# First layer of a graph network: edge attributes in 512-byte parts, products in two row tiles of 64, PSUM in units of four tiles

## The chip, the cores and the metric

The kernel runs on one core of one Trainium2 chip. The metric is device time in microseconds (us) of one execution. The engines are named as in the profile: PE is TensorE's matrix multiplication and PEld its loading of weights, DVE is VectorE, ACT is ScalarE, POOL is GpSimd, SP is SyncE. Each of them works through its own queue in order, and SP, ACT and POOL also issue DMA transfers from their queues.

## The reference

Four layers follow one another on 6250 nodes of 256 features, with 106250 edges that are sorted by their destination (dst):

```
edge_index = stack([src, dst])
x = x + L0_gnn(layernorm(x), edge_index, edge_attr_256)
x = x + L0_ffn(layernorm(x))      # attention over a fixed graph picks 2 of 4 experts
x = x + L1_gnn(layernorm(x), edge_weight, src, dst)
x = x + L1_ffn(layernorm(x))

def L0_gnn(x, (row, col), edge_attr):
    h = relu(concat([x[row], edge_attr], axis=1) @ W1 + b1)      # 106250 x 512 by 512 x 256
    agg = segment_sum(h, col) / max(count(col), 1)
    return relu(concat([x, agg], axis=1) @ W2 + b2)
```

All of it is float32. The change concerns nearly nothing but L0_gnn, which the text calls the first layer.

## The kernel before

The first layer splits W1. The node half of the product, y = layernorm(x) @ W1a + b1, is computed once for each node and stored in DRAM (y_dram), between the start and about 110 us. The edge half runs in a loop over edges: h = relu(y[src] + edge_attr @ W1b), and the sums per destination come from products with matrices of ones and zeros (equals) that compare the edge's destination with the node's number.

**Tiling.** There are T = 49 windows of P = 128 nodes. As the edges are sorted, a window's edges lie together: from a start found at run time (`start_of`, L1087) the kernel takes CW x P = 18 x 128 = 2304 edge rows, in 18 tiles of 128. They are worked through in NG = 3 groups (TURNS, L949) of G1 = 6 tiles, in two runs of NT = 3 tiles (k = g and k = g + 3). So there are 147 groups, and the loop over them (L1738 to L1771) is the first layer's loop.

**The steps of a group.** `load_attr` (L1494) loads the attributes of the 6 tiles into `ea` with 8 DMAs of 96 KB, 4 from SP's queue and 4 from ACT's. Each fills 32 partitions with pieces of 64 features, 256 bytes. Three `ea` buffers exist (L1455). `load_sources` (L1603) issues six indirect gathers from POOL, one for each tile, of y rows by source index into `h`, a ring of four groups. `turn` (L1611) transposes `ea` on DVE in blocks of 32 x 32 into `et`, so that features lie on partitions. `hidden(q, j)` (L1619) multiplies two tiles of `et` with W1b (`w1b`) over 128 rows in two steps of accumulation, into `ph`, a PSUM tile of 6 x 256 floats a partition (three banks, two such buffers). A float32 matmul shows as two in the trace, so a group has 24 ph matmuls. `join` (L1629) adds PSUM and `h` on DVE (L1632) and takes the relu on ACT (L1633), once a group. `add_up` (L1636) forms the sums per node with matmuls of 32 columns each (L1652, tile `pe`), four of which lie side by side in the array; a window's three turns show 12, 16 and 24 of them.

**The end of a window.** `end_of` (L1658 to L1710) is a generator whose stages are spread over the iterations that follow the window: division by the count (`rc` on DVE, ACT L1665), two transposes on PE (`pt<-ident,o`, L1158) that ACT empties (L1159), four products with W2, the residual and the layer norm on DVE and ACT, two transposes of the result into `b_all` (again L1158 and L1159), and products with `wgx` for the next layer's attention, which ACT copies into `gtab` and `a_dst` (L1704 to L1706). All of these use one PSUM buffer, `pt`.

**The order.** `Ordered.pin` (L28) ties every instruction of the loop to the one before it on the same engine, so that each engine keeps the program's order. One iteration q issues, in this order: join(q-1), hidden(q, 0), side work (sorting of edges for the middle layers), add_up(q-2) and a stage of end_of, gathers (LATE1 tiles of q+1, EARLY1 tiles of q+2), turn(q+1), hidden(q, 2), side work, the equality matrices, hidden(q, 4), the index work of later windows (`load_windows`, L1182), and at the end load_attr of up to q+4. The first groups' load_attr is issued in the stage before (L1557).

**Indices.** `load_windows` writes the gathers' indices. For windows from the third on, rows outside the window get an index of 8192 or more (FAR), and every gather is issued with a test (`bounds_check`) that skips such rows.

**Later stages.** Attention and experts run from about 1625 to 3080 us, the last layer's loop of gathers (`hg`, 831 of them) to the end. The last layer's pool opens at L2455 with 17 loads of weights on SP's queue (L2466 to L2489), ahead of the last stores and loads of the layer before it that use that queue.

Of the kernel before, what the change touches and what calls it, by code (L numbers as in the profile page):

```python
# [9 lines left out]
F32 = mybir.dt.float32  # L10
# [18 lines left out]
class Ordered:  # L29

    def __init__(self, tc):
        self.tc, self.last = tc, {}
        self.traced = tc.nc.cur_bb.bb.instructions
        self.at = self.traced[-1]

    def pin(self):
# [6 lines left out]
        for i in reversed(new):  # L43
            if i.engine in self.last:
# [867 lines left out]
def kernel(ctx: ExitStack, tc: tile.TileContext, a: dict, out: bass.AP):  # L912
# [25 lines left out]
    FAR = 8192.0  # L938
# [56 lines left out]
    with ExitStack() as fast:  # L995
# [180 lines left out]
        def gather(dst, table, idx, **more):  # L1176
# [5 lines left out]
        def load_windows(b, pool):  # L1182
# [47 lines left out]
            if first:  # L1230
                V.tensor_copy(flat3(src1[:, 0:first, :, :]), g[:, 0:first, :])
            far = g[:, first:, :]
            V.scalar_tensor_tensor(
                far, flat3(inside[:, first:, :, :]), -FAR, far, op0=OP.mult, op1=OP.add
            )
            V.tensor_scalar(
                flat3(src1[:, b * TB + first : (b + 1) * TB, :, :]), far, FAR, None, op0=OP.add
            )
# [92 lines left out]
        def make_keys(ix):  # L1331

            n = C2 // KS
            for k in range(KS):
                src, dst = (v.bitcast(I32)[:, k * n : (k + 1) * n] for v in (key, order))
                d, ok, last = (
                    ix.tile([P, n], t, name=f"key{i}", bufs=1) for i, t in enumerate((F32, F32, BF16))
# [110 lines left out]
        with ExitStack() as layer:  # L1448
# [8 lines left out]
            def load_weights(pool):  # L1457

                w1b = wp.tile([P, 2, D], F32, name="w1b")
                for k in range(4):  # L1460
                    rows = a["L0_gnn_W1"][D + 2 * k * Q : D + 2 * (k + 1) * Q, :]
# [32 lines left out]
            def load_attr(q):  # L1494

                w, g = groups1[q]
                ea = wea.tile([P, 2, NT * 4, 2 * Q], F32, name="ea")
                r = start_of(w, mybir.EngineType.Activation)
                rows = a["edge_attr_256"][bass.ds(r, WE), :]
                for i, k in enumerate((g, g + NG)):  # L1500
                    part = rows[k * NT * P : (k + 1) * NT * P, :]
                    for c in (0, 2, 1, 3):
                        (SY if c < 2 else SC).dma_start(
                            ea[c * Q : (c + 1) * Q, i, :, :],
                            part[:, 2 * c * Q : 2 * (c + 1) * Q].rearrange(
                                "(m p) d -> p m d", p=Q
                            ),
                        )
                return ea


            with (
# [11 lines left out]
                for t0, t1 in parts0:  # L1524
# [32 lines left out]
                    if b >= 4:  # L1557
                        ahead[b - 4] = load_attr(b - 4)
# [3 lines left out]
            with (  # L1562
                tc.tile_pool(name="e1", bufs=2) as wk,
                tc.tile_pool(name="y0", bufs=1) as wy,
                tc.tile_pool(name="ph1", bufs=2, space=PSUM) as psh,
# [4 lines left out]
                ring = [wy.tile([P, G1, HS], F32, name=f"h{i}") for i in range(4)]  # L1570
                for h in ring:
                    V.memset(h[:, :, D:WS], 1.0)
# [27 lines left out]
                def rows_of(q):  # L1600
# [1249 lines left out]
```

## Time and profile before

| what | value |
|---|---|
| runs | 4302.15, 4324.18, 4345.13 us; median 4324.18 |
| profiled execution | 4332.62 us, its span 4330.8 us, granted PE clock 0.824 |
| first layer's loop | about 110 to 1600 us |
| attention and experts | about 1625 to 3080 us |
| last layer's loop | 3080 to 4331 us |
| busy over the span | PE 3249.3, PEld 2483.7, DVE 2191.0, ACT 1189.9, POOL 2298.0 us |
| DMA packets | 698661, 423.05 MB, 532488 of them under 512 bytes |
| attribute loads | 588 on SP and 588 on ACT, 96 KB each |

Times in the views are microseconds from the span's start unless marked ns. A line of groups gives the source line, the engine and operation, the tile that is written and those that are read, the shapes and the count; then busy time and mean duration; then the idle time of the engine just before these instructions, and what ended it. "remote" and "another core or an unknown queue" mark a releaser that the profile can't name; "issue" is time in which an engine waited for nothing that the profile shows. In a timeline, the bracket is the idle time before a piece and its releaser. ACTq and SPq are the queues of ACT and SP issuing DMAs. PEclk is the clock granted to PE as a share of full speed.

### The profile page before, as it was taken

Reading aid. Unit: us, or ns where it says so; the run is one execution under the profiler, and the core shown is the slowest. Engines: PE = TensorE matmul, PEld = TensorE weight load, DVE = VectorE, ACT = ScalarE, POOL = GpSimd, SP = SyncE. Lnnn points to the kernel's source line nnn. Section 1 sums busy time; section 2 is a strip of 40 time slices with the busy share of each in tenths; the row PEclk is TensorE's granted clock in tenths of the full one; section 3 lists DMA queues with packets and bytes.
Section 4 is the critical chain, followed back from the end, with each engine's and each line's share of the span. In section 5 each row is a group of like instructions: output and inputs, shape, how many; then the busy total and the mean of one; then the engine's idle time right before and its main releaser. Section 6 shows DMA issues by size and latency. Waiting matters only on the chain.

```text
span 4330.8 us, 59911 instructions
## 1 busy us (share of the span) xinstructions
PE 3249.3 (75%) x18517; PEld 2483.7 (57%) x18517; DVE 2191.0 (51%) x6402; ACT 1189.9 (27%) x2200; POOL 2298.0 (53%) x2720
## 2 busy tenths in 40 slices
PE   7778788878888885777887878685356776777787
PEld 5556566656666664556666656564244454555566
DVE  6566566666565543555555454575123333333344
ACT  3122222222222231334544444464001111111133
POOL 2655555655666544345454444432666666665551
PEclk9889898989999897888898988896566777667687
DMA  6666667766776642222323232333111111111110
GB/s 187 156 145 148 144 151 155 159 140 152 160 168 152 149 119 61 63 63 81 97 77 104 68 101 70 87 103 93 46 46 51 47 50 50 51 50 47 49 49 20
DMA packets 698661, 423.05 MB, mean 98 GB/s; under 512 B 532488, under 2 KB 641092, under 8 KB 698332
## 3 DMA queue, kind: packets, MB, share of 16 engines
q1 hardware_dynamic: 366524, 188.25, 16.1%
q0 software_dynamic: 88512, 171.34, 16.1%
q10 hardware_dynamic: 243296, 59.53, 7.0%
q8 instruction: 150, 2.46, 0.2%
q14 instruction: 179, 1.47, 0.1%
HBM read 382.75 MB, written 42.50 MB: 98 GB/s over the span
## 4 chain that ended last, share of the span: by engine, by line
PE 49%; another core or an unknown queue 17%; issue 14%; DVE 9%; ACT 4%; POOL 3%; DMA 2%; ACTq 1%; SPq 1%; DVEq 0%; POOLq 0%
PE ph L1164 22%; PE py L1164 10%; PE pe L2710 5%; PE pe L1652 3%; PE pt L1164 3%; PE po L2031 2%; POOL hg L1177 1%; DVE et L1614 1%; POOL h L1177 1%; PE pt L1158 1%; DVE h L1632 1%; PE pa L1954 1%; DMA h<-y_dram,src 1%; DVE eq L2687 1%
## 5 line engine op out<-in xcount | busy, mean ns | idle before, releaser
L1177 POOL DMA_INDIRECT h<-y_dram,src x882 | 896.8, 1017 | 672.7 <-issue 318.4
L1177 POOL DMA_INDIRECT hg<-hp_dram,src x831 | 785.8, 946 | 489.4 <-issue 217.9
L1177 POOL DMA_INDIRECT sg<-gat_dram,src x612 | 595.3, 973 | 729.1 <-DVE pay L1991 308.5
L1164 PE MATMUL ph<-w1b,et 128*128 128x256 f32 x3528 | 885.2, 403 | 44.0 <-issue 29.6
L1164 PEld LDWEIGHTS ph<-w1b,et 128*128 128x128 f32 x3528 | 690.9, 201 | 224.7 <-issue 131.0
L1164 PE MATMUL py<-w,hh 128*128 128x256 f32 x1568 | 452.3, 427 | 96.6 <-issue 43.7
L2710 PEld LDWEIGHTS pe<-eq,hg 128*128 128x128 f32 x2036 | 380.5, 258 | 250.7 <-issue 157.2
L2710 PE MATMUL pe<-eq,hg 128*128 128x96 f32 (+15 forms) x2036 | 391.7, 338 | 147.2 <-issue 83.5
L1164 PE MATMUL ph<-b_all,w 128*128 128x256 f32 (+1 forms) x1600 | 470.4, 434 | 12.1 <-issue 11.0
L1632 DVE TENSOR_TENSOR h<-ph,h 128x1536 f32<-128x1536 f32 x147 | 258.3, 1757 | 421.2 <-remote 184.3
L2687 DVE TENSOR_SCALAR eq<-px,dst,ew 128x96 f32<-128x96 f32 x831 | 261.9, 368 | 311.0 <-remote 137.0
L1164 PEld LDWEIGHTS py<-w,hh 128*128 128x128 f32 x1568 | 305.6, 209 | 159.3 <-issue 58.5
L1633 ACT ACTIVATE h<-h 128x1536 f32<-128x1536 f32 x147 | 218.4, 1486 | 623.0 <-DMA ea<-in_edge_attr_dram 273.7
L1164 PEld LDWEIGHTS ph<-b_all,w 128*128 128x128 f32 x1600 | 324.1, 219 | 63.1 <-issue 21.0
L2009 DVE TENSOR_SCALAR E<-nodes,bits 128x256 bf16<-128x256 bf16 (+5 forms) x612 | 187.2, 338 | 181.3 <-remote 78.8
L1614 DVE STREAM_TRANSPOSE et<-ea 128x1536 f32<-128x1536 f32 x147 | 260.8, 1774 | 14.5 <-issue 9.3
L1832 ACT ACTIVATE hh<-ph,b 128x256 f32<-128x256 f32 (+1 forms) x400 | 166.6, 466 | 299.8 <-remote 153.1
L1652 PE MATMUL pe<-h,eq 128*32 128x257 f32 x2496 | 227.6, 430 | 26.0 <-issue 24.9
L1164 PE MATMUL py<-ew,g 65*128 65x256 f32 x392 | 138.2, 479 | 73.3 <-DVE x_all L2663 17.7
L1158 PE MATMUL pt<-ident,o 128*128 128x128 f32 x196 | 48.0, 334 | 164.1 <-ACT a_dst L1706 90.3
L2031 PE MATMUL po<-pays,E 128*128 128x61 bf16 x2116 | 119.1, 198 | 55.4 <-issue 45.1
L2031 PEld LDWEIGHTS <-E 128*128 128x128 bf16 x2116 | 104.1, 102 | 89.3 <-issue 67.8
(358 smaller groups left out, 4020.6 us busy)
## 6 DMA issues: line engine op xcount, KB each, us to landing
ea<-in_edge_attr_dram SPq DMA_DIRECT2D x588, 96.0 KB
ea<-in_edge_attr_dram ACTq DMA_DIRECT2D x588, 96.0 KB
w<-in_L_ffn_W_dram SPq DMA_DIRECT2D x48, 512.0 KB
y<-ys SPq DMA_DIRECT2D x96, 256.0 KB
rb<-low_dram SPq DMA_DIRECT2D x84, 256.0 KB
h<-y_dram,src POOLq DMA_INDIRECT x882
hg<-hp_dram,src POOLq DMA_INDIRECT x831
gtab<-y SPq DMA_DIRECT2D x100, 128.0 KB
```

The lines of the kernel that those rows point to most:

```text
L1158: TE.transpose(pt[:, c, :], src[:, c * P : (c + 1) * P], ident)
L1164: TE.matmul(dst, lhs(c), rhs(c), start=c == 0, stop=c == n - 1)
L1177: GP.indirect_dma_start(out=dst, out_offset=None, in_=table[0:NP, :], in_offset=IndirectOffsetOnAxis(ap=idx, axis=0), **more,)
L1614: V.transpose(et[q].rearrange("p c m k -> p m c k"), ahead.pop(q).rearrange("p i m (c k) -> p (i m) c k", c=2),)
L1632: V.tensor_add(h, ph.pop(q), h)
L1633: SC.activation(h, h, AF.Relu)
L1652: TE.matmul(sums[w][b * Q : (b + 1) * Q, :], equals[of][k][:, t, (b - lo) * Q : (b - lo + 1) * Q], rows_of(of)[:, j, 0:WS], start=start, s ...
L1832: SC.activation(hidden[u][:, f, :n, :], ph[:, f - f0, :n, :], AF.Gelu, bias=b1[:, e, f : f + 1],)
L2009: V.tensor_scalar(Es[g, j][:, 0:n, :].rearrange("p b k -> p (b k)"), nodes16[:, 0 : n * P], bits.bitcast(F32)[:, g * G + j : g * G + j + 1 ...
L2031: TE.matmul(pos[g][bank][:, to * HP : (to + 1) * HP], E[:, b - b0, :], pays[g % 2][:, j, :], start=bank not in begun, stop=bank not in lat ...
L2687: V.tensor_scalar(equals[k][:, j, :], lanes[:, 0:NW], dst_of[:, t : t + 1], ew[:, t : t + 1], op0=OP.is_equal, op1=OP.mult,)
L2710: TE.matmul(sums[b][:, lo - t0 * P : hi - t0 * P], hg[:, j, :], eq[:, j, lo - n0 : hi - n0], start=False, stop=after >= (t0 + n) * P,)
```

## The change

- **Attributes.** `load_attr` makes 4 DMAs of 192 KB a group, not 8 of 96 KB: each fills 32 partitions with pieces of 128 features, 512 bytes. SP issues the two of the first run of tiles, ACT the two of the second. They are put on a list, and `issue` takes two from it at each of three points of an iteration: after the gathers, after hidden(q, 1), and at the end.
- **Products.** `et` and `w1b` now lie so that the tiles of the first run have their features on partitions 0 to 63 and those of the second run on 64 to 127. `hidden(q, n)` multiplies one tile of each run, over 64 rows in four steps of accumulation, in turns, each into a PSUM bank of its own. A group shows 48 ph matmuls, with as many loads of weights; each streams 256 columns as before.
- **Units.** A `ph` tile holds four tiles (two of each run) in two banks, with three buffers. `join(u)` works on such a unit, 221 in all, and stands inside `hidden` at the start of the next unit. The ring `h` is one tile of 24 rows, as large as before.
- **Gathers.** Only the last two of a window's 18 tiles (SKIP = 16), in windows from the third on, are gathered with the test and with FAR indices. The others gather all 128 rows.
- **Last layer.** A second `Ordered`, for SP's queue alone, keeps the 17 weight loads behind what SP issued before them in the program.

Besides, three scratch tiles got fixed names. The diff, with its unchanged lines cut:

```diff
@@ -28,10 +28,15 @@
-    def __init__(self, tc):
-        self.tc, self.last = tc, {}
+    def __init__(self, tc, *engines):
+        self.tc, self.last, self.engines = tc, {}, engines
         self.traced = tc.nc.cur_bb.bb.instructions
         self.at = self.traced[-1]
+        for engine in engines:
+            self.last[engine] = next(
+                i.name for i in reversed(self.traced)
+                if i.engine == engine and "Boundary" not in type(i).__name__
+            )
@@ -41,6 +46,8 @@
         for i in reversed(new):
+            if self.engines and i.engine not in self.engines:
+                continue
             if i.engine in self.last:
@@ -935,7 +942,7 @@
     CW = 18
-    FAR = 8192.0
+    SKIP, FAR = CW - 2, 8192.0
     WE = CW * P
@@ -1173,7 +1180,8 @@
-        def gather(dst, table, idx, **more):
+        def gather(dst, table, idx, skipping=False):
+            more = {"bounds_check": N - 1, "oob_is_err": False} if skipping else {}
             GP.indirect_dma_start(
@@ -1227,15 +1235,12 @@
             first = 2 if b == 0 else 0
-            if first:
-                V.tensor_copy(flat3(src1[:, 0:first, :, :]), g[:, 0:first, :])
-            far = g[:, first:, :]
+            far = g[:, first:, SKIP:]
             V.scalar_tensor_tensor(
-                far, flat3(inside[:, first:, :, :]), -FAR, far, op0=OP.mult, op1=OP.add
+                far, flat3(inside)[:, first:, SKIP:], -FAR, far, op0=OP.mult, op1=OP.add
             )
-            V.tensor_scalar(
-                flat3(src1[:, b * TB + first : (b + 1) * TB, :, :]), far, FAR, None, op0=OP.add
-            )
+            V.tensor_scalar(far, far, FAR, None, op0=OP.add)
+            V.tensor_copy(flat3(src1[:, sl, :, :]), g)
...
@@ -1456,9 +1462,10 @@
-                w1b = wp.tile([P, 2, D], F32, name="w1b")
+                w1b = wp.tile([P, 4, D], F32, name="w1b")
                 for k in range(4):
-                    rows = a["L0_gnn_W1"][D + 2 * k * Q : D + 2 * (k + 1) * Q, :]
+                    half = D + (k % 2) * P
+                    rows = a["L0_gnn_W1"][half : half + P, :]
                     SY.dma_start(
@@ -1494,19 +1501,26 @@
                 w, g = groups1[q]
-                ea = wea.tile([P, 2, NT * 4, 2 * Q], F32, name="ea")
+                parts = []
+                ea = wea.tile([P, NT * 4, P], F32, name="ea")
                 r = start_of(w, mybir.EngineType.Activation)
                     part = rows[k * NT * P : (k + 1) * NT * P, :]
-                    for c in (0, 2, 1, 3):
-                        (SY if c < 2 else SC).dma_start(
-                            ea[c * Q : (c + 1) * Q, i, :, :],
-                            part[:, 2 * c * Q : 2 * (c + 1) * Q].rearrange(
-                                "(m p) d -> p m d", p=Q
-                            ),
-                        )
-                return ea
+                    for c in range(2):
+                        at = (2 * i + c) * Q
+                        parts.append((
+                            SY if i == 0 else SC,
+                            ea[at : at + Q, :, :],
+                            part[:, c * P : (c + 1) * P].rearrange("(m p) d -> p m d", p=Q),
+                        ))
+                return ea, parts
+
+            def issue(parts, n):
+
+                for engine, to, part in parts[:n]:
+                    engine.dma_start(to, part)
+                del parts[:n]
@@ -1555,21 +1569,22 @@
                     if b >= 4:
-                        ahead[b - 4] = load_attr(b - 4)
+                        ahead[b - 4], parts = load_attr(b - 4)
+                        issue(parts, len(parts))
                 tc.tile_pool(name="y0", bufs=1) as wy,
-                tc.tile_pool(name="ph1", bufs=2, space=PSUM) as psh,
+                tc.tile_pool(name="ph1", bufs=3, space=PSUM) as psh,
                 tc.tile_pool(name="pe1", bufs=1, space=PSUM) as pse,
-                ring = [wy.tile([P, G1, HS], F32, name=f"h{i}") for i in range(4)]
-                for h in ring:
-                    V.memset(h[:, :, D:WS], 1.0)
+                NH = 4 * G1
+                ring = wy.tile([P, NH, HS], F32, name="h")
+                V.memset(ring[:, :, D:WS], 1.0)
                 equals, et, ph, sums = {}, {}, {}, {}
@@ -1597,41 +1612,50 @@
-                def rows_of(q):
-                    return ring[q % len(ring)]
+                def row(q, j):
+                    return (2 * (NT * q + j % NT) + j // NT) % NH
                         if j in some:
-                            gather(rows_of(q)[:, j, 0:D], y_dram, src1[:, w, k, t : t + 1],
-                                   bounds_check=N - 1, oob_is_err=False)
+                            gather(
+                                ring[:, row(q, j), 0:D], y_dram, src1[:, w, k, t : t + 1],
+                                w > 1 and k * NT + t >= SKIP,
+                            )
-                    et[q] = wk.tile([P, 2, G1 * 4, Q], F32, name="et")
+                    et[q] = wk.tile([P, 4, NT * 4, Q], F32, name="et")
                     V.transpose(
                         et[q].rearrange("p c m k -> p m c k"),
-                        ahead.pop(q).rearrange("p i m (c k) -> p (i m) c k", c=2),
-                    )
-
-                def hidden(q, j):
-                    if j == 0:
-                        ph[q] = psh.tile([P, G1, D], F32, name="ph")
-                    for i in range(j, j + 2):
-                        mm(
-                            ph[q][:, i, :],
-                            lambda c: et[q][:, c, i * 4 : (i + 1) * 4, :].rearrange("p m k -> p (m k)"),
-                            lambda c: w1b[:, c, :],
-                        )
-
-                def join(q):
-
-                    h = rows_of(q)[:, :, 0:D]
-                    V.tensor_add(h, ph.pop(q), h)
+                        ahead.pop(q).rearrange("p m (c k) -> p m c k", c=4),
+                    )
+
+                def hidden(q, n):
+
+                    u, k = divmod(NT * q + n, 2)
+                    if k == 0:
+                        if u:
+                            join(u - 1)
+                        ph[u] = psh.tile([P, 2, 2, D], F32, name="ph")
+                    for c in range(4):
+                        for i in range(2):
+                            at = slice(2 * i * Q, 2 * (i + 1) * Q)
+                            m = et[q][at, c, n * 4 : (n + 1) * 4, :].rearrange("p m k -> p (m k)")
+                            TE.matmul(ph[u][:, i, k, :], m, w1b[at, c, :], start=c == 0, stop=c == 3)
+
+                def join(u):
+
+                    n = min(2, NT * NQ1 - 2 * u)
+                    at = 4 * u % NH
+                    h = ring[:, at : at + 2 * n, 0:D]
+                    V.tensor_add(
+                        h.rearrange("p (n i) d -> p i n d", i=2), ph.pop(u)[:, :, :n, :],
+                        h.rearrange("p (n i) d -> p i n d", i=2),
+                    )
                     SC.activation(h, h, AF.Relu)
-                    et.pop(q)
@@ -1641,7 +1665,7 @@
                             TE.matmul(
-                                sums[w], equals[q][k][:, t, :], rows_of(q)[:, j, 0:WS],
+                                sums[w], equals[q][k][:, t, :], ring[:, row(q, j), 0:WS],
                                 start=turn == 0 and j == 0, stop=turn == NG - 1 and j == G1 - 1,
@@ -1652,7 +1676,7 @@
                                 equals[of][k][:, t, (b - lo) * Q : (b - lo + 1) * Q],
-                                rows_of(of)[:, j, 0:WS], start=start, stop=stop,
+                                ring[:, row(of, j), 0:WS], start=start, stop=stop,
                             )
@@ -1738,10 +1762,11 @@
                 turn(0)
+                LOT = 2
                 ordered = Ordered(tc)
                 for q in range(NQ1 + 2):
-                    if 0 < q <= NQ1:
-                        join(q - 1)
+                    if q == NQ1:
+                        join((NT * NQ1 - 1) // 2)
                     if q < NQ1:
@@ -1753,18 +1778,22 @@
                         load_sources(q + 2, EARLY1)
+                    issue(parts, LOT)
                     if q + 1 < NQ1:
                         turn(q + 1)
+                    for n in range(q + 2, min(q + 5, NQ1)):
+                        if n not in ahead:
+                            ahead[n], more = load_attr(n)
+                            parts += more
                     if q < NQ1:
-                        hidden(q, 2)
+                        hidden(q, 1)
+                    issue(parts, LOT)
                     steps(keys or (sort if q % 4 else []))
                         equals[q] = equal(wk, *groups1[q])
-                        hidden(q, 4)
+                        hidden(q, 2)
                     steps(slow)
-                    for n in range(q + 2, min(q + 5, NQ1)):
-                        if n not in ahead:
-                            ahead[n] = load_attr(n)
+                    issue(parts, LOT)
                     ordered.pin()
@@ -2443,6 +2472,7 @@
                 run(routing, False)
+        ordered = Ordered(tc, mybir.EngineType.SP)
         experts.close()
@@ -2462,6 +2492,7 @@
         ):
+            ordered.at = ordered.traced[-1]
             w2t = wp.tile([P, D], F32, name="w2t")
@@ -2495,6 +2526,7 @@
             )
+            ordered.pin()
             g2s = [wp.tile([EH2 + 1, NX, BT, P], F32, name=f"g2_{i}") for i in range(2)]
                 GP.memset(g2[last, :, :, :], 1.0)
```

More of the change, by code (lines that the diff above doesn't have):

```diff
@@ L1336, in make_keys @@
                 d, ok, last = (
-                    ix.tile([P, n], t, name=f"key{i}", bufs=1) for i, t in enumerate((F32, F32, BF16))
+                    ix.tile([P, n], t, name=m, bufs=1)
+                    for m, t in (("key0", F32), ("key1", F32), ("lt", BF16))
                 )
```

## The prediction

> **What bounds the kernel now.** I read the windows first, to see which stage the change touches. The first layer's loop runs from about 110 to 1600 us. Its inner stretches look alike:
>
> ```profile
> core 0: us, PE busy (x) PEld busy (x) DVE busy (x) ACT busy (x) POOL busy (x), PEclk, DMA share, GB/s
> 600.00:900.00 300.00, 249.33 (x1406) 184.49 (x1406) 194.69 (x382) 66.42 (x107) 181.31 (x178) 0.92 0.70 155
> ```
>
> PE is busy 83% of the stretch, DVE 65%, POOL 60%, ACT 22%, and the 16 DMA engines 70%. So PE is the nearest bound. From 110 to 1600 it is busy 1218.76 of 1490 us: if every idle moment went, 271 us would go. The groups by form of 130 to 1600 say what PE does, and what stops it:
>
> ```profile
> L1164 PE MATMUL ph<-w1b,et 128*128 128x256 f32 x3472 | 869.2, 402 | 33.8 <-issue 29.6 <-DVE et L1614 1.9 <-DVE ln_rs L1689 1.7
> L1164 PEld LDWEIGHTS ph<-w1b,et 128*128 128x128 f32 x3471 | 678.0, 201 | 209.5 <-issue 118.1
> L1652 PE MATMUL pe<-h,eq 128*32 128x257 f32 x2484 | 224.4, 430 | 19.5 <-issue 18.4
> L1158 PE MATMUL pt<-ident,o 128*128 128x128 f32 x190 | 46.8, 336 | 163.9 <-ACT a_dst L1706 90.3 <-remote 61.4 <-ACT gtab L1705 7.2
> ```
>
> The edge products (ph) are 71% of PE's time, and they hardly wait. The wait sits at pt: the transpose that opens the end of the next window needs the PSUM buffer that ACT empties into gtab and a_dst (90.3 + 61.4 + 7.2 = 158.9 us, 3.4 per window). PE's timeline of one window shows it:
>
> ```profile
> 739.63 1.51 PE L1652 MATMUL pe<-h,eq 128*32 128x257 f32 x24
> 741.07 0.92 PE L1164 MATMUL ph<-w1b,et 128*128 128x256 f32 x3
> 742.56 2.97 PE L1164 MATMUL ph<-w1b,et 128*128 128x256 f32 x13 [0.58 <-issue]
> 745.36 0.52 PE L1164 MATMUL pt<-wgx,b_all 128*128 128x24 f32 x4
> 745.73 1.97 PE L1164 MATMUL ph<-w1b,et 128*128 128x256 f32 x8
> 750.63 0.69 PE L1158 MATMUL pt<-ident,o 128*128 128x128 f32 x2 [2.93 <-ACT a_dst L1706]
> 751.25 1.94 PE L1652 MATMUL pe<-h,eq 128*32 128x257 f32 x12
> ```
>
> PE stands 2.93 us here (7.34 in the window before), and what follows runs slower: 12 pe in 1.94 us, where 24 took 1.51. ACT's timeline of the same stretch says why a_dst was late:
>
> ```profile
> 737.35 2.50 ACTq L1503 DMA_DIRECT2D ea<-in_edge_attr_dram  x3
> 740.13 1.48 ACT L1633 ACTIVATE h<-h 128x1536 f32<-128x1536 f32 x1 [3.40 <-DMA ea<-in_edge_attr_dram]
> 742.66 0.39 ACT L1159 ACTIVATE b_all<-pt 128x256 f32<-128x256 f32 x1 [1.05 <-remote]
> 745.51 0.47 ACT L1665 ACTIVATE o<-pe,rc 128x256 f32<-128x256 f32 x1 [2.46 <-remote]
> 750.26 0.18 ACT L1704 ACTIVATE gtab<-pt 128x16 f32<-128x16 f32 x1 [4.28 <-remote]
> ```
>
> ACT's queue is held by attribute loads (2.50 us), so relu, b_all and all behind it come late; then gtab starts 4 us after its matmuls were recorded, with a releaser that the profile can't name. The waits of 130 to 1600, and the DMA queues of 600 to 900, complete it:
>
> ```profile
> ACT h L1633 <- DMA ea<-in_edge_attr_dram: 243.7, 68, 9.6
> ACT gtab L1704 <- remote: 220.0, 38, 9.3
> ```
>
> ```profile
> q0 software_dynamic: 8544, 22.09, 29.9%
> q10 hardware_dynamic: 49824, 11.98, 20.3%
> q1 hardware_dynamic: 48756, 12.06, 19.8%
> ```
>
> The attribute queues q1 and q10 move 24 MB in 256-byte pieces at 40% of the engines' time (12.5 GB/s an engine); the gathers (q0) move nearly as much in 30% (15.4).
>
> **The change, part by part.** The sum is made against the profiled execution, 4332.6 us; the median of the runs, 4324.2, is 8.4 lower.
>
> 1. Two row tiles. 24 matmuls over 128 rows become 48 over 64, in pairs that can run side by side. The row now: 24 ph in 5.38 us back to back, 0.224 each. A pair at 0.224 costs nothing; one after the other it would be 0.448, 3528 x 0.224 = +790 us. No row tile is in this trace. The nearest row is pe, in four column tiles: 24 in 1.51 us, 0.063 each, against 0.224 / 4 = 0.056 if perfect, a loss of 12% for four. I take 6% for two, 0.0125 a pair: 3528 x 0.0125 = +44. A gain is excluded, since the same columns stream. Ends 0 and +790.
>
> "TensorE: Matmul & The Clock Gate" of the Trainium skill (Part 3, Measured speedup vs the span model) gives 3.07 times for four row tiles, not four, and its section on LDWEIGHTS says that a load goes by columns and not by rows, so half as many rows save nothing: both speak against this change. An estimate by 3.07 of 4 for each pair (0.292 us) would make term 1 +240 and the sum 4461.
>
> 2. Changes of tile mode. Transposes and the window's own matmuls over 128 rows now stand between row tiles: ph to pt, two around the w2 block, one before the second transposes, two around gtab's matmuls, six more per window, 288. Where the mode changes now (pe to ph), the second ph starts 0.32 us after the first instead of 0.22: 0.10 each, +29. PEld's idle there, 0.41, is the upper end, +118; the lower is 0.
>
> 3. The stall of each window. ACT and SP issue two attribute loads a group each, not four, a load waits for the one issued eight before it, whose semaphore it reuses (two groups back, no longer one), and pieces of 512 bytes halve the packets. What can go: the 158.9 us, and the cold work after them (1.94 - 0.76 for 12 pe, 0.69 - 0.38 for pt, 4.10 - 3.58 for the next 16 ph: 2.0 us x 47 = 94), 253 together. I take half, -126: the 2.50 us of ACT's queue are nearly a stall of 2.93, while the unnamed lateness (1.05 + 2.46 + 4.28) is only partly the DMA engines' load; I saw it where their share stood near 1.0 (741 to 746) and not where it was 0.4 (760 to 765). Ends 0 and -253; the other sign I exclude, as no load is issued earlier or bigger in sum. When this wait goes, the next that is late is the join on gathers, then PE itself.
>
> 4. Start of the loop. ACT is held by 12 attribute issues for 20.57 us from 87.23, the first relu waits 30.07 and the second join 14.21 for gathers behind those packets. With half the issues: -12, ends 0 and -20.
>
> 5. Last layer. SP issues its 17 weight loads after the loads and stores on which x_all and hp_dram wait, not before (2965.7 to 2976): -3, ends 0 and -6 (what lies between the first weight issue and the gathers at 2998 that DVE's own work does not fill). The weights come late for DVE's first use, which the gathers' 1.25 us each cover.
>
> 6. Costed at nothing. 220 joins of 1024 elements for 147 of 1536: by 1757 ns for 1536 and 418 for 256, 1.2 us each, 270 us for 258, under DVE's 35% idle; if the cover went, +12. ACT likewise, 1.04 us x 220 = 229 for 218. A join now comes within its group and can find an EARLY gather missing, but it was issued over a group before. Gathers without the bounds test: 946 ns (hg) against 1017, up to -56 of POOL, which has 586 idle; the rows now fetched beyond a window are at most those of its last two tiles, which keep the test. Attribute issues in the middle of an iteration stand in SP ahead of nothing but edge windows, and in ACT behind relu. Three index operations on DVE per block: under 7 us, hidden.
>
> Sum: +44 + 29 - 126 - 12 - 3 = -68: 4265 against the profiled execution, 4256 as the median.
>
> "DMA: Bandwidth & Descriptors" (Issuing engines are not separate DMA queues) says that the time a sequencer takes to issue is usually small. This trace differs: 2.50 us here. By that rule half of term 3 falls away, and the sum would be 4328.
>
> **Rivals.**
>
> A, the forecast: pairs side by side, half the stall gone. 4256; with all of term 3 and perfect pairs 4332.6 + 29 - 253 - 20 - 6 - 8 = 4075.
>
> B, no difference: the lateness isn't the loads' doing, and only half of ACT's 2.50 us per window is saved (47 x 1.25 = -59). 4332.6 + 73 - 59 - 15 - 8 = 4324. For it: the lateness stands also where ACT had nothing in its queue (gtab at 750.26). Against it: 243.7 us of relu's waits end on those loads.
>
> C, slower: weight loads bound the pairs. A load of 128 columns takes 190 ns; if the two of a pair go one after the other, a pair takes 0.38 us, +0.156 x 3528 = +550, PE's work is 1219 + 550 + 29 = 1798 against a loop of 1490: with no idle left +308, so 4332.6 + 308 - 15 - 8 = 4618, with today's idle less term 3 (145) 4763. It decides from a pair of 0.256 us on (112 us / 3528 = 0.032 above 0.224), and from 0.268 it is over 1% slower. For it: twice as many loads, and no row here shows that a load of fewer rows is shorter. Against it: pe's 24 loads of 118 ns fit in 1.51 us, so about two ran at once in different tiles.
>
> **How the numbers follow.** A 0.60, B 0.15, C 0.25. A measurement of this kernel tells about 1% from no change (43 us; the three runs lie within 0.5% of the median): A is faster, B the same, C slower. A's own range is 4110 to 4281. The range goes from 4090 (bound 4075, little below it) to 4480, which takes in pairs of 0.292 us and leaves out the worse half of C.
>
> **What would show it.** Term 1: 48 ph of one group in 5.4 to 5.8 us, pairs starting together; over 6.2 is C. Term 2: gaps around pt of 0.1 us. Term 3: ACT's wait on DMA ea below 100 us, pt's waits below 80, DMA share near 0.57. Term 4: the second join before 125 us. Wrong would be: pt's waits unchanged with ACT free (B), PE's busy share over 90% with a longer loop (C), or joins waiting on gathers for more than today's 184.3.

## The result and the profile after

The changed kernel takes 4500.13 us (median of 5 runs, 4488.62 to 4510.52), the kernel before 4320.66 us beside it: ratio 1.0421 (95% interval 1.0369 to 1.0472). It was forecast at 4256 us, 1.6% faster, and is 4.2% slower. The profiled execution has a span of 4498.3 us against 4330.8. The last window's sums start at 1778.7 us, not 1602.0, so the first layer lost 177 us; everything behind it gained 9 (2719.6 against 2728.8).

The same kernel before took 4220 to 4334 us on four chips of the experiments, and 3327 to 3329 on two others, so each experiment is compared with the kernel before on its own chip.

The window of 600 to 900 us of the changed kernel, columns as before:

```profile
core 0: us, PE busy (x) PEld busy (x) DVE busy (x) ACT busy (x) POOL busy (x), PEclk, DMA share, GB/s
600.00:900.00 300.00, 241.18 (x1804) 164.22 (x1800) 168.32 (x340) 58.97 (x109) 148.69 (x154) 0.88 0.55 133
```

The DMA engines' share fell from 0.70 to 0.55, as hoped, but so did the work: 133 GB/s for 155, 154 POOL instructions for 178. No engine became the bound; everything waits more. The groups of 130 to 1700:

```profile
L1647 PE MATMUL ph<-w1b,et 64*128 64x256 f32 x6629 | 897.8, 411 | 52.4 <-issue 50.7
L1647 PEld LDWEIGHTS ph<-w1b,et 64*128 64x128 f32 x6630 | 682.8, 202 | 254.6 <-issue 159.1 <-PE pe L1676 11.9 <-DVE h L1654 1.7
L1676 PE MATMUL pe<-h,eq 128*32 128x257 f32 x2392 | 255.6, 449 | 42.8 <-issue 39.3 <-DMA h<-y_dram,src 1.6 <-DVE h L1654 0.5
L1165 PE MATMUL pt<-ident,o 128*128 128x128 f32 x180 | 48.5, 358 | 121.8 <-ACT a_dst L1730 74.1 <-remote 18.9 <-issue 9.0
```

Twice the ph matmuls cost nearly the same busy time: the pairs run side by side. The loss is elsewhere: pe waits 42.8 us, where it waited 19.5, and pt still waits 121.8 (163.9 before). PE's timeline shows both:

```profile
805.38 5.45 PE L1647 MATMUL ph<-w1b,et 64*128 64x256 f32 x48
810.77 0.44 PE L1165 MATMUL pt<-ident,o 128*128 128x128 f32 x2
811.14 0.96 PE L1676 MATMUL pe<-h,eq 128*32 128x257 f32 x3
812.43 0.42 PE L1676 MATMUL pe<-h,eq 128*32 128x257 f32 x2 [0.34 <-issue]
813.14 0.38 PE L1676 MATMUL pe<-h,eq 128*32 128x257 f32 x1 [0.29 <-issue]
813.84 1.49 PE L1676 MATMUL pe<-h,eq 128*32 128x257 f32 x18 [0.33 <-issue]
815.26 3.72 PE L1647 MATMUL ph<-w1b,et 64*128 64x256 f32 x32
818.91 0.62 PE L1171 MATMUL pt<-wgx,b_all 128*128 128x24 f32 x4
819.47 2.00 PE L1647 MATMUL ph<-w1b,et 64*128 64x256 f32 x16
826.71 0.69 PE L1165 MATMUL pt<-ident,o 128*128 128x128 f32 x2 [5.24 <-ACT a_dst L1730]
```

48 ph take 5.45 us. Then PE crawls: pe starts at 811.14, 812.43, 813.14, 813.84, one or two matmuls each 0.7 us, with nothing that the profile shows to wait for. And gtab's matmuls are recorded at 818.91, yet ACT's timeline has:

```profile
814.13 0.38 ACT L1166 ACTIVATE b_all<-pt 128x256 f32<-128x256 f32 x1 [3.66 <-PE pe L1676]
816.85 1.06 ACT L1658 ACTIVATE h<-h 128x1024 f32<-128x1024 f32 x1 [2.34 <-DVE h L1654]
817.84 0.47 ACT L1689 ACTIVATE o<-pe,rc 128x256 f32<-128x256 f32 x1
826.34 0.18 ACT L1728 ACTIVATE gtab<-pt 128x16 f32<-128x16 f32 x1 [8.03 <-remote]
```

ACT's queue is empty and it waits 8.03 us for a matmul long recorded. The semaphore events in the trace, from which the profile infers what ended a wait, say why. From 793 to 807 us each update of PE follows its matmul's recorded end by 0.01 to 0.03 us; then one comes 0.74 us late, none arrives until 813.9, when five come within 0.3 us, and the one for gtab's matmuls (end 819.54) comes at 826.32, just ahead of ACT's start. From 600 to 1500 us, PE had an update outstanding for over 0.3 us in 328 of 900 us (380 before). These two sums take for each matmul the next event on record; as 3361 of PE's 3706 updates are on record, they are estimates.

The waits of 130 to 1700, some of 130 to 1780 (the whole loop), and the DMA queues of 600 to 900:

```profile
ACT h L1658 <- DVE h L1654: 407.8, 117, 22.0
ACT gtab L1728 <- remote: 156.4, 24, 9.1
```

```profile
PE pt L1165 <- ACT a_dst L1730: 78.5, 27, 5.6
PE pt L1165 <- remote: 18.9, 4, 4.9
PE pt L1165 <- ACT gtab L1729: 3.3, 1, 3.3
ACT h L1658 <- DMA ea<-in_edge_attr_dram: 26.7, 6, 6.2
DVE h L1654 <- remote: 228.2, 47, 8.6
```

```profile
q0 software_dynamic: 7468, 19.20, 25.7%
q10 hardware_dynamic: 21408, 10.17, 14.6%
q1 hardware_dynamic: 20756, 10.09, 14.3%
```

ACT's wait on attribute loads fell from 243.7 to 26.7 us and their share from 40% to 29%. What the forecast took for the cause was removed. The transposes' wait for gtab and a_dst did fall with it, from 158.9 to 100.7 us (78.5 + 18.9 + 3.3), but not to nothing, and it isn't what made the kernel slower. The joins' wait on unnamed releasers rose from 184.3 to 228.2.

### The profile page after: what moved, and what is told of

Its sections match the earlier page's. It is cut to its first block, busy times and chain, and to the rows that moved or that the text cites. A ratio compares the mean times of both kernels' runs of the same rounds, so it can differ in the third digit from the quotient of the medians.

```text
span 4498.3 us, 64090 instructions
## 1 busy us (share of the span) xinstructions
PE 3390.9 (75%) x22045; PEld 2520.0 (56%) x22045; DVE 2198.1 (49%) x6479; ACT 1204.3 (27%) x2274; POOL 2255.5 (50%) x2720
## 4 chain that ended last, share of the span: by engine, by line
PE 55%; another core or an unknown queue 19%; issue 10%; DVE 8%; ACT 4%; DMA 2%; POOL 1%; SPq 0%; DVEq 0%; ACTq 0%; POOLq 0%
PE ph L1647 15%; PE ph L1171 11%; PE py L1171 11%; PE pt L1171 4%; PE pe L1676 4%; PE pe L2742 4%; PE po L2060 1%; PE pt L1165 1%; DVE h L1654 1%; DMA h<-y_dram,src 1%; DVE eq L2719 1%; DVE et L1631 1%; PE pa L1983 1%; PE pm L1171 0%
## 5 line engine op out<-in xcount | busy, mean ns | idle before, releaser
L1185 POOL DMA_INDIRECT h<-y_dram,src x882 | 853.4, 968 | 892.7 <-issue 442.6
L1647 PE MATMUL ph<-w1b,et 64*128 64x256 f32 x7056 | 957.7, 411 | 71.2 <-issue 65.3
L1647 PEld LDWEIGHTS ph<-w1b,et 64*128 64x128 f32 x7056 | 728.5, 202 | 286.7 <-issue 185.9
L1654 DVE TENSOR_TENSOR h<-ph,h 128x1024 f32<-128x1024 f32 (+1 forms) x221 | 267.5, 1210 | 505.1 <-remote 228.2
L1658 ACT ACTIVATE h<-h 128x1024 f32<-128x1024 f32 (+1 forms) x221 | 233.3, 1056 | 746.6 <-DVE h L1654 457.8
L1676 PE MATMUL pe<-h,eq 128*32 128x257 f32 x2496 | 266.8, 448 | 45.2 <-issue 41.6
L1676 PEld LDWEIGHTS pe<-h,eq 128*32 128x32 f32 x2496 | 93.9, 121 | 169.4 <-issue 149.9
L1171 PE MATMUL ph<-b_all,ew 128*128 128x512 f32 (+2 forms) x256 | 111.2, 560 | 52.2 <-ACT g L2655 24.1
```

The source lines that it names most:

```text
L1171: TE.matmul(dst, lhs(c), rhs(c), start=c == 0, stop=c == n - 1)
L1185: GP.indirect_dma_start(out=dst, out_offset=None, in_=table[0:NP, :], in_offset=IndirectOffsetOnAxis(ap=idx, axis=0), **more,)
L1647: TE.matmul(ph[u][:, i, k, :], m, w1b[at, c, :], start=c == 0, stop=c == 3)
L1654: V.tensor_add(h.rearrange("p (n i) d -> p i n d", i=2), ph.pop(u)[:, :, :n, :], h.rearrange("p (n i) d -> p i n d", i=2),)
L1658: SC.activation(h, h, AF.Relu)
L1676: TE.matmul(sums[w][b * Q : (b + 1) * Q, :], equals[of][k][:, t, (b - lo) * Q : (b - lo + 1) * Q], ring[:, row(of, j), 0:WS], start=start, ...
```

## The experiments

Theory after the result: PE's updates come late whatever the traffic, and twice the instructions make PE crawl. Rivals: units and joins, place of the loads, the 512-byte parts, changes of tile mode, DMA traffic.

**Four kernels on a chip where the kernel before takes 3328.55 us.** First the changed kernel with 256-byte parts and full rows (all edits are cut to their main lines):

```diff
-ea = wea.tile([P, NT * 4, P], F32, name="ea")      # 4 loads, 512 bytes
+ea = wea.tile([P, 2, NT * 4, 2 * Q], F32, name="ea")   # 8 loads, 256 bytes
-    TE.matmul(ph[u][:, i, k, :], m, w1b[at, c, :], start=c == 0, stop=c == 3)   # 64 rows, 4 steps
+    mm(ph[u][:, i, k, :], lambda c: et[q][:, c, ...], lambda c: w1b[:, c, :])   # 128 rows, 2 steps
```

> The changed kernel with the attributes in 256-byte parts (8 loads a group) and the products over 128 rows, 24 matmuls a group, as before; units of four tiles, the order of the loads, the gathers and the last layer stay as changed. Theory (PE's twofold number of instructions lets its semaphore updates fall behind, and PE crawls): the whole loss goes, 4260 to 4330 us, and no crawl in the pe matmuls. Rival 1 (the loss comes from units of four tiles, the joins between products, or the gathers without the test): 4450 to 4510. Rival 2 (changes of tile mode cost it): as the theory in time, but the pe matmuls would have crawled only next to a change of mode.

Measured 0.991 (0.9889 to 0.9931). Row tiles kept, 256-byte parts:

```diff
-for c in range(2): ... ea[at : at + Q, :, :], part[:, c * P : (c + 1) * P]
+for c in range(4): ... ea[at : at + Q, :, half], part[:, 2 * c * Q : 2 * (c + 1) * Q]
```

> The changed kernel with its attribute loads in pieces of 256 bytes, 8 loads of 96 KB a group; row tiles stay. Theory (PE's instructions): DMA is not the bound, so within 1% of the changed kernel, 4460 to 4545. Rival (transfers hold PE's updates up, and the 512-byte pieces gained something that the rest lost): 4560 to 4700.

Measured 0.9981 (0.9972 to 0.9991). Without the attribute loads of the loop, and without its gathers:

```diff
-ahead[n], more = load_attr(n); parts += more
+ahead[n] = kept[n % 3]
```

> The changed kernel without the attribute loads in the loop: the first three groups' attributes are used for all groups, so the loads of 144 groups are left out. Theory (PE's instructions): the late updates and the crawl stay, 4420 to 4500. Rival (DMA traffic holds PE's updates up): 4150 to 4300, and gaps of PE above 600 ns in the pe matmuls mostly gone.

```diff
-load_sources(q + 1, LATE1) ... load_sources(q + 2, EARLY1)
```

> The changed kernel without the gathers of the loop (those of the first three groups stay; later groups add to what lies in the ring), so 864 of 882 gathers are left out. Theory (PE's instructions): crawl and late updates stay, 4400 to 4500. Rival (the gathers' transfers hold PE's updates up; q0 moved 102 GB/s while updates were late and 46 otherwise): 4100 to 4300, and PE's updates come at once.

0.9932 (0.9913 to 0.9952) and 0.9939 (0.992 to 0.9959). None of the expected times holds, because the kernel before is 1000 us faster here, and in the trace of the 256-byte version no update of PE is over 0.3 us late from 600 to 1200. Chips like this one are called chips where updates come at once, the others chips with late updates. The ratios still say something: where updates come at once full rows gain 0.9%, row tiles give 0.7% of it back, and transfers hardly matter.

**The two kernels themselves, on another such chip** (before 3327.03 us).

> The changed kernel itself, beside the kernel before on the same chip, because the chip of the four runs ahead of this showed the kernel before at 3329 us, not 4321, and none of the late updates. If the loss of 4.2% belongs to the late updates (theory), then on a chip without them the change is not slower: 0.985 to 1.000 of the kernel before, since its version with 256-byte parts was 0.998. If the row tiles cost it everywhere (rival): 1.02 or more.

> The kernel before itself, for its trace on this chip. Theory: if this chip shows it near 3329 us, PE is busy over 90% in the first layer's loop, no update of PE comes more than 0.3 us late, and the waits on remote releasers before gtab and the joins are gone; if it shows it near 4321, they are all there. The ratio is 1.00 by construction, within 0.3%.

The changed kernel: 0.9966 (0.9952 to 0.998), the theory's case. The kernel before: 0.9999 (0.9988 to 1.0009). The rows of 600 to 900, first the kernel before, then the changed one:

```profile
600.00:900.00 300.00, 282.25 (x1744) 219.19 (x1743) 232.62 (x440) 82.17 (x137) 227.69 (x222) 0.98 0.96 192
```

```profile
600.00:900.00 300.00, 297.89 (x2716) 222.18 (x2713) 241.66 (x472) 89.85 (x162) 222.58 (x229) 1.00 0.89 197
```

Here the change does what it was meant to: PE is busy 297.89 of 300 us at full clock, and its loop ends at 1272.7 us instead of 1295.6. The DMA engines are 89 to 96% busy, more than where updates come late, and no update of the changed kernel is over 0.3 us late from 300 to 1200 us (of 878 of the kernel before 5 are, at most by 1.96): their load as such isn't the cause. PE's timeline of the changed kernel:

```profile
602.42 5.45 PE L1647 MATMUL ph<-w1b,et 64*128 64x256 f32 x48
607.80 0.44 PE L1165 MATMUL pt<-ident,o 128*128 128x128 f32 x2
608.17 1.51 PE L1676 MATMUL pe<-h,eq 128*32 128x257 f32 x24
609.61 3.72 PE L1647 MATMUL ph<-w1b,et 64*128 64x256 f32 x32
```

The same 48 ph in 5.45 us, and 24 pe in 1.51 without a crawl. Neither row tiles nor changes of mode crawl by themselves.

**Joins and loads, and half of the products, on a chip with late updates** (before 4221.48 us). Full rows with joins by group, and with the loads at the iteration's end:

```diff
-if k == 0: join(u - 1); ph[u] = psh.tile([P, 2, 2, D])     # bufs=3
+if n == 0: join(q - 1); ph[q] = psh.tile([P, G1, D])       # bufs=2
```

> The full-row version with mid-iteration loads (256-byte parts, 128 rows), but joins once a group of six tiles, with two PSUM buffers of three banks, as before. Where PE's updates come at once: if units of four tiles made the 0.9% that this version gains over the kernel before, then 0.998 to 1.002; if the loads' place did (theory, since ACT's queue no longer blocks), then 0.988 to 0.994. Where updates come late: 0.97 to 1.01, as PE has as many instructions as before.

```diff
-issue(parts, LOT)          # at three points of the iteration
+ahead[n], parts = load_attr(n); issue(parts, len(parts))   # at its end
```

> The full-row version with units of four tiles, but all eight attribute loads of a group at the end of the iteration, in the order of before. Where PE's updates come at once: 0.997 to 1.001 if the loads' place made the gain (theory), 0.988 to 0.994 if the units did. Where updates come late: 0.97 to 1.01.

1.019 (1.0133 to 1.0246), above its expectation, and 1.0049 (1.0022 to 1.0077). With joins by group, gtab's wait on unknown releasers is 249.4 us from 300 to 1500, with units 54.0: which speaks for units of four, though the place of the loads differs too. The changed kernel with half of its products left out:

```diff
-for c in range(4):
+for c in range(2):         # stop=c == 1
```

> The changed kernel with half of the products left out (two of the four steps of accumulation), so that PE has 24 matmuls of 64 rows a group: as many instructions as before, half the streaming. Where PE's updates come at once: PE no longer bounds the loop, which goes to the gathers (1.3 us each, 7.8 a group): 3315 - 147 x 0.4 to 0.6, 3220 to 3270. Where they come late: with the theory (the number of PE's instructions makes the loss) the crawl goes, 4150 to 4330; if the mode changes or joins make it, 4400 to 4500.

0.9872 (0.9798 to 0.9946): time as the theory had it, but the crawl did not go (2.85 us per window, table below).

**Full rows, changed, and row tiles with the loads at the end, side by side on a chip with late updates** (before 4230.45 us). The third is the changed kernel with the edit shown above for loads at the end.

> The version with 128 rows and 256-byte parts, all else as changed (0.991 on a chip where PE's updates came at once), again, to stand beside the changed kernel on one chip. Updates at once: 0.989 to 0.993. Updates late: with the theory (row tiles double PE's instructions, and that makes the loss) 0.99 to 1.01; with the rival (the loads and units in the middle of the iteration make the loss) 1.03 to 1.05.

> The changed kernel again, beside the one with full rows and the one with loads at the end. Updates at once: 0.995 to 0.998. Updates late: 1.03 to 1.05, by either theory.

> The changed kernel with the four attribute loads of a group at the end of the iteration, as before; row tiles and units stay. Updates at once: as the changed kernel, 0.994 to 0.999, since PE has no waits left there. Updates late: with the theory (PE's instructions) 1.03 to 1.05, with the rival (place of the loads) 1.00 to 1.02.

1.0026 (1.0002 to 1.005), 1.044 (1.04 to 1.0481) and 1.0443 (1.0415 to 1.0471). The loss is reproduced. It belongs to the row tiles with their 512-byte parts, and neither to the units, the gathers' test and the last layer, nor to the place of the loads.

**Number of instructions or row tiles, on a chip with late updates** (before 4220.19 us). Full rows with half of the products left out; the same with each matmul split in two; the changed kernel with half of its products left out, again.

```diff
-mm(ph[u][:, i, k, :], ...)
+TE.matmul(ph[u][:, i, k, :], m, w1b[:, 0, :], start=True, stop=True)                 # unsplit
+for n2 in range(2): TE.matmul(ph[u][:, i, k, half], m, w1b[:, 0, half], start=True, stop=True)  # split
```

> The full-row version with half of the products left out: 12 matmuls of 128 rows and 256 columns a group. Updates late: with the theory (the number of PE's instructions sets the loss, not its streaming) 4 to 6% below the version with half products in row tiles, 0.93 to 0.95 of the kernel before; with the rival (row tiles themselves, their changes of mode, cost it) also 0.93 to 0.96: the next kernel tells the two apart. If streaming sets it: equal to that version, 0.98 to 1.00. Updates at once: 0.95 to 0.98, the gathers bound the loop.

> As the one before, half of the products left out, but each matmul split into two of 128 columns: 24 matmuls of 128 rows a group, as many instructions as half products in row tiles, with no row tile in the loop. Updates late: theory (number of instructions) within 1.5% of the version in row tiles, 0.97 to 1.00 of the kernel before; rival (row tiles) as the unsplit one, 0.93 to 0.96. Updates at once: up to 1% above the unsplit one, as 24 loads of 190 ns are 4.6 us a group and PE is not the bound.

> The changed kernel with half of its products left out, again (0.987 on a chip with late updates), to stand beside the two others on one chip. Updates late: 0.98 to 0.995. Updates at once: 0.96 to 0.98, within 1% of the other two.

0.9821 (0.9784 to 0.9858), 0.9913 (0.9884 to 0.9943), 0.9884 (0.9853 to 0.9915). The theory's 4 to 6% is missed: doubling the instructions costs 0.9% here, row tiles 0.6%. The split kernel's PE timeline:

```profile
617.60 0.65 PE L1678 MATMUL pe<-h,eq 128*32 128x257 f32 x4
618.60 0.39 PE L1678 MATMUL pe<-h,eq 128*32 128x257 f32 x1 [0.35 <-issue]
620.00 1.07 PE L1678 MATMUL pe<-h,eq 128*32 128x257 f32 x11 [1.01 <-issue]
```

It crawls without a row tile in its loop: gaps over 0.6 us within ph or pe come 121 times from 300 to 1450 us, in the row tiles 138 and 130 times (the two runs), in the unsplit kernel 58 times. So here the crawl goes with the number of PE's instructions. But PE has room to spare (211 of 300 us busy in the split kernel), and its loss in the loop may be partly covered.

**Parts and traffic, on a chip with late updates** (before 4333.84 us): the 256-byte parts with row tiles, no attribute loads, and no gathers in the loop, again.

> The changed kernel with 256-byte parts, row tiles kept, again. Updates late: if the row tiles make the loss (theory), 1.03 to 1.05; if the 512-byte parts do (rival), 1.00 to 1.01. Updates at once: 0.997 to 0.999.

> The changed kernel without the attribute loads of the loop, again. Updates late: if transfers make PE's updates late (rival), below 0.93, crawl and stalls mostly gone; if they come late whatever the traffic (theory), 1.00 to 1.05. Updates at once: 0.99 to 0.996.

> The changed kernel without the gathers of the loop, again. Updates late: rival (the gathers' transfers, 102 GB/s while updates were late against 46 otherwise, hold them up) below 0.93; theory 1.00 to 1.05. Updates at once: 0.99 to 0.996.

1.0489 (1.0424 to 1.0554): the row tiles make the loss, not the 512-byte parts. Without the attribute loads 1.0225 (1.015 to 1.0301): a part of the loss goes, but PE still has an update outstanding in 314 of the 900 us from 600 to 1500 (376 in the kernel with 256-byte parts). Without the gathers 0.9265 (0.9196 to 0.9334), the rival's side: the theory that updates come late whatever the traffic falls. The row of 600 to 900 and PE's timeline without the gathers:

```profile
600.00:900.00 300.00, 297.97 (x2701) 222.24 (x2700) 240.85 (x474) 89.49 (x158) 0.00 (x0) 1.00 0.42 103
```

```profile
611.11 5.45 PE L1648 MATMUL ph<-w1b,et 64*128 64x256 f32 x48
616.49 0.44 PE L1165 MATMUL pt<-ident,o 128*128 128x128 f32 x2
616.85 1.51 PE L1677 MATMUL pe<-h,eq 128*32 128x257 f32 x24
618.29 3.72 PE L1648 MATMUL ph<-w1b,et 64*128 64x256 f32 x32
```

With the gathers gone the loop runs on this chip as on those where updates come at once: PE 297.97 of 300 us, full clock, no crawl, and no update over 0.3 us late from 300 to 1200. The attribute loads still run beside it. So PE's updates come late only while the loop gathers; what in a gather holds them up is not shown.

PE's time per window, in us, from the starts of its matmuls and the granted clock in the traces. Whole windows are counted, from one window's gtab matmuls to the next's, between 300 and 1500 us (to 1150 for the three kernels with windows under 24 us, to 1450 for half of the products). Crawl is gaps above 0.6 us between two ph or two pe, stall such gaps elsewhere (each less 0.22), cold is half of the time at half clock outside these gaps, and rest is what remains.

| kernel, updates | window | crawl | stall | cold | rest |
|---|---|---|---|---|---|
| before, late | 30.59 | 1.21 | 4.71 | 2.03 | 22.64 |
| changed, late | 34.04 | 2.56 | 4.24 | 2.91 | 24.33 |
| full rows, late | 29.41 | 1.11 | 4.13 | 1.48 | 22.69 |
| 256-byte parts, row tiles, late | 34.85 | 3.48 | 3.87 | 3.22 | 24.28 |
| no attribute loads, same chip as the row above | 32.41 | 1.90 | 4.18 | 2.10 | 24.23 |
| no gathers, same chip | 23.54 | 0.00 | 0.14 | 0.00 | 23.39 |
| half, full rows, late | 27.78 | 1.90 | 7.57 | 3.44 | 14.88 |
| half, split, late | 28.53 | 2.96 | 6.28 | 3.68 | 15.62 |
| half, row tiles, late (first, again) | 28.64, 28.53 | 2.85, 2.61 | 5.92, 6.13 | 3.80, 3.57 | 16.07, 16.22 |
| before, at once | 23.87 | 0.29 | 0.89 | 0.26 | 22.43 |
| changed, at once | 23.54 | 0.00 | 0.15 | 0.00 | 23.39 |

Without gathers, the changed kernel on a chip with late updates has the same window, 23.54 us, as with them on a chip without.

The gaps of the crawl lie mostly where updates are out: in the changed kernel 67% of their time falls into the 37% of 300 to 1500 us in which an update of PE was outstanding for over 0.3 us, in the kernel before 81% into 41%. Another cause would be that PE's instructions arrive late, as more of them have to be loaded. The trace speaks against it: a packet of the two DMA queues that the profile calls instruction (q8 and q14) was in flight during, or up to 0.5 us before, 12 of the changed kernel's 126 such gaps, where gaps moved to random places would give 24.

## Why the prediction was wrong

**Term 3 failed**, in the step "ACT's queue is held by attribute loads" and "the unnamed lateness is only partly the DMA engines' load". It priced -126 us, half of the 158.9 us for which the transposes waited on gtab and a_dst and of the cold work after them. ACT was freed and the DMA share fell. The transposes' wait lost 58 us, but their other waits grew (on dst, start and ix_g, 21.6 to 52.6 us over the loop), so that all stalls together went from 4.71 to 4.24 us per window, -23 for 49 windows; and cold work, which was to shrink, rose by 43. The unnamed lateness at gtab is that of PE's updates, and it comes with the gathers, which the change keeps, all but the test on most of them: on one chip the stall is 4.18 us per window without the attribute loads and 0.14 without the gathers, and the ratio 0.9265 without gathers where row tiles with them have 1.0489. Rival B had this right, that the lateness isn't the loads' doing, though not the time. The two instants that the prediction compared, 741 to 746 and 760 to 765, were no evidence on the share of DMA: where updates come at once it stands at 0.9 throughout.

**A term was missing.** A late update was taken for a delay of others only. While updates are out PE also crawls, and the change doubles PE's instructions for the products. Crawl rose from 1.21 to 2.56 us per window (+66 us over 49), cold work from 2.03 to 2.91 (+43), the rest from 22.64 to 24.33 (+83, of which 47 also show where updates come at once, and the other 36 are not traced). With the stall's -23 that is 169 of the 177 lost. That row tiles make the loss, and that it needs the gathers, is shown. That the crawl goes with the number of instructions is shown by the split kernel, with half of the products; that this number alone makes the whole 4.2% is not shown, since there it cost 0.9%, where 4 to 6% were expected, and no run splits the matmuls of the full work. That PE has no room in the full work to hide the crawl in is argued only, and so is how a late update holds PE's next matmuls.

**Term 1 was right**, and even too dear: 48 ph take 5.45 us, where 24 took 5.38 to 5.45: about 0 us and not +44. The 3.07 of four in "TensorE: Matmul & The Clock Gate" of the Trainium skill (Part 3, Measured speedup vs the span model), and the +240 estimated from it, do not show with two tiles: they reach 2.0, and no run here has four. Rival C had the sign but the wrong mechanism: a load of half the rows is no shorter (202 ns for 201), but the two of a pair fit into its step.

**Term 2**: 0.09 us per change (ph to pt 0.31 us from start to start for 0.22), 288 of them 26 us. Priced 29, the right size for the changes themselves; the whole rest of a window grew by 0.96 us where updates come at once, 47 us in all, so what came along with them was left out.

**Term 4** gave nothing: ACT's second relu starts at 134.99 us after a wait of 21.96, where it stood at 133.45 before, though a join is now four tiles, not six.

**Term 5** can't be told from the spread. Behind the first layer it is 9 us less on the chip of the result and 3.6 on the other (2036.2 for 2039.8), but four kernels with the same last layer differ by 4.6 us there on one chip (2035.6 to 2040.2).

**Term 6** held: DVE 2198.1 us for 2191.0, ACT 1204.3 for 1189.9, neither the bound.

**The issue time.** "DMA: Bandwidth & Descriptors" of the Trainium skill (Issuing engines are not separate DMA queues) calls the time of issuing usually small relative to the DMA itself. The prediction set ACT's 2.50 us for three issues against it without that comparison, so it didn't show that the trace differs. Where the loads are issued made no difference to the row tiles, 1.044 in the middle or 1.0443 at the end of the iteration; the time of issuing itself no run tests.

## What to carry to other kernels

A wait whose releaser the profile can't name is not to be put down to the traffic that happens to run beside it: compare when the releasing engine's work was recorded with when its update came, and take out each kind of traffic in turn. Where updates of an engine come late, that engine's number of instructions can have a price of its own: with half of the products, twice the matmuls of half the columns cost 0.9%. Row tiles were free in streaming but cost 0.96 us per window around their changes of mode where updates come at once, so the version with full rows and the rest of the change is the better one where updates come at once (0.991 against 0.9966), and where they come late no version here beat the kernel before (1.0026 at best with all the work done).

## What the runs showed of the hardware

Two row tiles of 64 rows, each in a PSUM bank of its own, ran fully side by side: 48 float32 matmuls of 256 columns took 5.45 us, as 24 over 128 rows do.

On some chips PE's semaphore updates arrive late while indirect gathers run: ACT waited up to 9.1 us on the unnamed releaser of gtab, and by the events on record an update came up to 9.3 us after its matmul's recorded end in the kernel before. On others the changed kernel shows none over 0.3 us with more traffic. While updates were out, the changed kernel's gathers moved 102 GB/s (600 to 1500 us), otherwise 46; where updates come at once they moved 95 all the time, so this rate alone isn't the cause. Why chips differ, and how a gather holds PE's updates up, stays open.
